# A two-layer decoder on one core: constants queued behind a norm, unread products at the start, and another split of the last stage

## The chip, the cores and the metric

The kernel runs on one core of a Trainium2 chip. The metric is the time of one execution on the device in microseconds (us), lower is better. TensorE is called PE here, VectorE DVE, ScalarE ACT, GpSimd POOL and SyncE SP, as in the profile. PEld is PE's weight load, and a q after a name (SPq) is the queue on which that engine issues transfers.

## The reference

Eight sequences of 128 tokens, 256 wide, pass through two decoder layers. Each layer has self-attention, cross-attention with a context, and a feed-forward, each followed by a residual and a norm without weights. Layer 0's feed-forward has 4-bit weights with low-rank additions; layer 1's is a mixture of 64 experts, of which each token takes the best 8.

```
x = _layernorm(x + _L0_attn_ref(x, Wq, Wk, Wv, Wo))          # 16 heads of 16, causal
x = _layernorm(x + _L0_xattn_ref(x, ctx, ...))
x = _layernorm(x + _L0_ffn_ref(x, ...))                      # 256 -> 1024 -> 256
x = _layernorm(x + _L1_attn_ref(x, w_qkv, w_o))              # 16 heads of 128
x = _layernorm(x + _L1_xattn_ref(x, ctx, ctx))               # 8 heads
x = _layernorm(x + _L1_ffn_ref(x, gate_w, w13, w2))          # 64 experts, the best 8 per token

_layernorm(x) = (x - mean(x)) / sqrt(var(x) + 1e-5)

_L1_ffn_ref(x):
    combine = weights of the 8 best experts of each token, from softmax(x @ gate_w.T)
    out = sum over experts e of combine[:, e] * (silu(x @ w13_e[:128].T) * (x @ w13_e[128:].T)) @ w2_e.T
```

## The kernel before, in words

All arithmetic of the products is in float32, which PE does in two passes; the profile shows each product as two records. The stages follow one another in the order of the reference, and within a stage a planner orders the instructions of DVE, ACT and POOL by priorities and estimated times of its own, while PE's order is mostly written out by hand. Every engine works through its own queue in order. An instruction that waits holds up all that stand behind it on its engine.

**Start.** SP issues the loads of weights and inputs, `wq` and `xT` first (`load`, L118). PE's first work is `project` (L286), which makes queries, keys and values of the first four sequences (tiles `l_p`) from `xT` and `wq`, `wkk`, `wv`. Then a pipeline of scores, softmax, transposes and weighing runs over sequences and head groups (L383). The softmax (L206) takes maxima on DVE (`nm_l`), exponentials on ACT (`l_e`), and scales on DVE (L220). The feed-forward's weights are made beside it: `dequantise` (L231) loads codes (`q_up`) and scales (`sc_up`), and a DVE step at L241 multiplies them to `w_up`.

**Feed-forward of layer 0.** `down` (L418) ends each sequence with a norm. `layernorm` (L173) takes statistics on DVE (`st`, `mv`), the root on POOL in two steps (`rsqrt_eps`, L167: an addition at L170 and a power at L171, tile `rs`), and the last step on DVE (L181). It returns the root's instruction; for the norms before the feed-forward these are kept in `roots`. `transposed` (L184) then turns the normed tiles on PE (`pt_l1a`) for layer 1, whose attention projects each head's q, k and v (L691).

After the feed-forward the program text names constants for routing and for layer 1's cross-attention, all made on POOL: `before`, `iota`, `starts`, `numbers`, `turns`, `rows_16`, `blks_16`, `seen`, and the two halves of `keys` (L602 to L640). In the text they stand behind the last norm. In POOL's queue the planner mixes them with it.

**Expert loop.** Tokens are sorted by expert, 104 visits of 128 columns each multiply with one expert's weights (L1093, L1110), and results go by indirect transfers to `pair_rows` in memory. In between, DVE makes `cw`, the eight weights of each token (`weight`, L1021), and `spread` (L1036) lays the first `ON_PE` = 6 of them on diagonals (`diag`).

**Tail.** After the loop, eight transfers of 1 MB on SP's queue bring back one sequence each as `z`, tokens by 8 results of 256. For each sequence, PE sums the first six results with the diagonals (`moe_sum`, L1176), DVE adds the last two to the residual (L1180) and then PE's sum to it (`moe_r`, L1182). `layernorm` makes `y`, and ACT's queue carries it out (L1185). `r` and `y` take turns in two buffers each of the pool `wk`.

Of the kernel before, what the change touches and what calls it, by code (L numbers as in the profile page):

```python
# [9 lines left out]
F32 = mybir.dt.float32  # L10
# [3 lines left out]
AF = mybir.ActivationFunctionType  # L14
ALU = mybir.AluOpType
AX = mybir.AxisListType

P = 128
B = 8
S = 128  # L20
D = 256
# [12 lines left out]
TOP = 8  # L34
NG = B * S * TOP // P
# [4 lines left out]
MIDDLE = (P - 1) / 2  # L40
# [19 lines left out]
def decoder_kernel(ctx: ExitStack, tc: tile.TileContext, i, out):  # L60
    nc = tc.nc
# [5 lines left out]
    wk = ctx.enter_context(tc.tile_pool(name="work", bufs=2))  # L67
    sm = ctx.enter_context(tc.tile_pool(name="small", bufs=4))
# [22 lines left out]
    def ps_o(name):  # L91
        return ps_of["o"].tile([P, 512], F32, tag="o", name=name)
# [74 lines left out]
    def rsqrt_eps(dst, var):  # L167

        n = dst.shape[1]
        nc.gpsimd.tensor_scalar(dst, var, EPS, None, ALU.add)  # L170
        return nc.gpsimd.tensor_tensor(dst, dst, minus_half[: dst.shape[0], :n], ALU.pow)  # L171

    def layernorm(dst, r, name):  # L173

        st = sm.tile([P, 6], F32, tag="ln_st", name=f"st_{name}")
        nc.vector.bn_stats(st, r)  # L176
        mv = sm.tile([P, 2], F32, tag="ln_mv", name=f"mv_{name}")
        nc.vector.bn_aggr(mv, st)  # L178
        rs = sm.tile([P, 1], F32, tag="ln_rs", name=f"rs_{name}")
        root = rsqrt_eps(rs, mv[:, 1:2])  # L180
        nc.vector.tensor_scalar(dst, r, mv[:, 0:1], rs, ALU.subtract, ALU.mult)  # L181
        return root.ins
# [23 lines left out]
    def softmax(e, s, name):  # L206
# [12 lines left out]
        for a in range(n):  # L219
            nc.vector.tensor_scalar(e[:, a, :], e[:, a, :], inv[:, a : a + 1], None, ALU.mult)  # L220

    w_up = fp.tile([P, 2, FF], F32, name="w_up")
# [50 lines left out]
    with l0, tc.tile_pool(name="l0a", bufs=2) as ap:  # L275
# [102 lines left out]
                project(1, 2 * b + jj)  # L378

        with tc.manual_schedule(engines={nc.tensor.engine}):  # L380
            for part in range(8):
                project(0, part)
            run_pipelined(  # L383
                [(b, jj) for b in range(B) for jj in range(2)], [scores, ahead, turn, weigh, add]
            )
# [8 lines left out]
    roots = []  # L394
# [23 lines left out]
    def down(b):  # L418
        h, bb = b // 4, b % 4
        xb = wk.tile([P, D], F32, tag="xb", name=f"xb_{b}")  # L420

        with tc.issue_after(roots[B - 1]):
            nc.gpsimd.tensor_tensor(xb, x2[b // 2][:, b % 2, :], b_down, ALU.add)
        ps = ps_o(f"down_{b}")
        for f in range(NF):
            nc.tensor.matmul(
                ps[:, :D], hT[h][:, f, bb * S : (bb + 1) * S], w_dn[:, f, :],
                start=(f == 0), stop=(f == NF - 1),
            )
        r = wk.tile([P, D], F32, tag="r", name=f"ff_r_{b}")  # L430
        nc.vector.tensor_tensor(r, ps[:, :D], xb, ALU.add)
        layernorm(x3[b // 2][:, b % 2, :], r, f"l0f_{b}")


    with tc.tile_pool(name="l0x", bufs=2) as ap, tc.manual_schedule(engines={nc.tensor.engine}):
# [149 lines left out]
    with tc.manual_schedule(engines={nc.tensor.engine}):  # L585
# [14 lines left out]
    rp = ctx.enter_context(tc.tile_pool(name="route", bufs=1))  # L600

    before = rp.tile([P, P], F32, name="before")  # L602
    nc.gpsimd.memset(before, 1.0)
    nc.gpsimd.affine_select(
        before, before, pattern=[[1, P]], compare_op=ALU.is_gt, fill=0.0, base=0, channel_multiplier=-1
    )
    iota = rp.tile([P, P], F32, name="iota")
    nc.gpsimd.iota(iota, pattern=[[1, P]], base=0, channel_multiplier=0, allow_small_or_imprecise_dtypes=True)
    starts = rp.tile([P, P], F32, name="starts")
    nc.gpsimd.iota(starts, pattern=[[P, P]], base=0, channel_multiplier=0, allow_small_or_imprecise_dtypes=True)  # L610

    numbers = rp.tile([P, B], F32, name="numbers")
    nc.gpsimd.iota(
        numbers, pattern=[[S, B]], base=0, channel_multiplier=1, allow_small_or_imprecise_dtypes=True
    )
    nc.gpsimd.tensor_scalar(numbers, numbers, 1.0 / (B * S), 1.0, ALU.mult, ALU.add)
    turns = rp.tile([P, TOP], F32, name="turns")
    nc.gpsimd.iota(turns, pattern=[[1, TOP]], base=0, channel_multiplier=0, allow_small_or_imprecise_dtypes=True)
    rows_16 = rp.tile([P, P, TOP], F16, name="rows_16")
    nc.gpsimd.iota(rows_16, pattern=[[1, P], [0, TOP]], base=0, channel_multiplier=0, allow_small_or_imprecise_dtypes=True)  # L620
    nc.gpsimd.tensor_scalar(rows_16, rows_16, -MIDDLE, None, ALU.add)
    blks_16 = rp.tile([P, NG, TOP], F16, name="blks_16")
    nc.gpsimd.iota(blks_16, pattern=[[1, NG], [0, TOP]], base=0, channel_multiplier=0, allow_small_or_imprecise_dtypes=True)
    comb = rp.tile([P, B, NE], F32, name="combine")
    seen = rp.tile([P, B, NE], F32, name="seen")
    nc.gpsimd.memset(seen[:, 0, :], 0.0)


    slot1 = rp.tile([P, B, NE], F32, name="slot1")


    keys_pool = ExitStack()
    kpool = keys_pool.enter_context(tc.tile_pool(name="l1k", bufs=1))
    keys = kpool.tile([P, B, 2, D], F32, name="keys")
    kept = []
    one_at = ident.rearrange("p (j two r) -> p two r j", two=2, r=16)
    for par in range(2):
        m = cp.tile([P, 1], F32, name=f"one_row_{par}")
        nc.vector.reduce_sum(m, one_at[:, 1 - par, 0, :], axis=AX.X)
        nc.gpsimd.tensor_scalar(keys[:, :, par, :], cx, quarter[par], m, ALU.mult, ALU.add)  # L640
        t = cp.tile([P, 1], F32, name=f"kept_{par}")
        nc.vector.tensor_tensor(t, m, rows_of[par], ALU.add)
        kept.append(t)


    x4 = new_stream("x4")
# [19 lines left out]
        layernorm(x4[b // 2][:, b % 2, :], r, f"l1a_{b}")  # L666

    def weigh(st, h, n):

        if n == L1_HEADS - 1:  # L670
            add_heads(4 * h, 0, n)
        ps = ps_o(f"l1_c_{h}_{n}")
        nc.tensor.matmul(ps, ones, st["p"].rearrange("p b k -> p (b k)"), start=True, stop=True)  # L673
        nc.vector.tensor_tensor(st["v"], ps, st["v"], ALU.mult)  # L674
        scaled[h, n] = st["v"]
        if n == L1_HEADS - 1:
            add_heads(4 * h, n, n + 1)
            if h == 0:
                for b in range(1, 4):
                    add_heads(b, 0, L1_HEADS)  # L680
# [349 lines left out]
        nc.vector.reduce_sum(cw[:, b, :], eq, axis=AX.X)  # L1030


    ON_PE = 6
    diag = dgp.tile([P, B, ON_PE, P], F32, name="diag")

    def spread(b):  # L1036
# [130 lines left out]
    zs = []  # L1167
    for b in range(B):
        z = tp.tile([P, TOP, D], F32, tag="z", name=f"z_{b}")
        nc.sync.dma_start(out=z, in_=zv[b])  # L1170
        zs.append(z)
    for b in range(B):
        z = zs[b]
        ps = ps_mm(f"moe_sum_{b}")[:, :D]
        for k in range(ON_PE):
            nc.tensor.matmul(ps, diag[:, b, k, :], z[:, k, :], start=(k == 0), stop=(k == ON_PE - 1))  # L1176

        acc = x5[b // 2][:, b % 2, :]
        for k in range(ON_PE, TOP):
            nc.vector.scalar_tensor_tensor(acc, z[:, k, :], cw[:, b, k : k + 1], acc, ALU.mult, ALU.add)  # L1180
        r = wk.tile([P, D], F32, tag="r", name=f"moe_r_{b}")
        nc.vector.tensor_tensor(r, ps, acc, ALU.add)  # L1182
        y = wk.tile([P, D], F32, tag="y", name=f"y_{b}")
        layernorm(y, r, f"l1f_{b}")
        nc.scalar.dma_start(out=out[b], in_=y)  # L1185


# [60 lines left out]
```

## Time and profile before

Three runs took 901.76, 903.53 and 905.52 us; the median is 903.53.

| | before |
|---|---|
| profiled execution, its own time | 903.73 us |
| its span | 901.9 us |
| PE busy | 820.6 us (91%) |
| DVE busy | 465.0 us (52%) |
| ACT busy | 287.8 us (32%) |
| POOL busy | 228.1 us (25%) |
| mean granted PE clock | 0.95 |
| bytes moved by transfers | 87.63 MB |

The span runs from the first instruction to the last, and the execution's own time has 1.8 us around it. Busy times are sums over stages with different limits, so the timeline of a stage tells more than the shares. A row of a timeline gives the start, the length, the engine, the line, the operation with its output and inputs, how many instructions it stands for, and in brackets how long the engine was idle before it and what ended that.

### The profile page before, as it was taken

To read this page: it belongs to the slowest core of one execution; us is meant where nothing else is said; L and a number is where in the kernel's file an instruction comes from. 1 tells how busy PE (TensorE), PEld (TensorE's weight loads), DVE (VectorE), ACT (ScalarE), POOL (GpSimd) and SP (SyncE) were. 2 spreads that over 40 slices of the span, in tenths; PEclk is the share of its full clock that TensorE was granted. 3 is DMA by queue.
4 is the path that set the end of the run, shared out by engine and by line. 5 is a ranking of instruction groups with operands and counts; after the bars stand their busy time and mean duration, and the time that the engine had idled before them with its cause. 6 is when DMAs were issued, how large, how long until landed. Compare 5 with 4: busy or idle time off the path is not lost. (4 is left out here: it accounts for less than half of the span.)

```text
span 901.9 us, 14220 instructions
## 1 busy us (share of the span) xinstructions
PE 820.6 (91%) x4560; PEld 545.3 (60%) x4560; DVE 465.0 (52%) x1304; ACT 287.8 (32%) x988; POOL 228.1 (25%) x311
## 2 busy tenths in 40 slices
PE   7998998999799999999999999997588888999845
PEld 3555454377455556855556755544488877888844
DVE  2999766431244443244444367665796333433325
ACT  2667353211233332033432033332232322333300
POOL 0010301231500000100005122201566655555522
PEclk9999978799899999999999999998599999999969
DMA  7500030080000000000001000000578888989573
GB/s 224 177 1 1 1 94 0 1 280 0 0 1 0 1 1 1 0 1 0 1 0 47 1 1 13 13 13 13 188 213 286 292 275 240 296 291 295 177 290 157
DMA packets 39105, 87.63 MB, mean 97 GB/s; under 512 B 6128, under 2 KB 15696, under 8 KB 38000
## 3 DMA queue, kind: packets, MB, share of 16 engines
q1 hardware_dynamic: 31728, 68.80, 23.7%
q0 software_dynamic: 6144, 16.79, 5.5%
q10 hardware_dynamic: 1152, 1.05, 0.3%
q8 instruction: 41, 0.67, 0.3%
q14 instruction: 40, 0.33, 0.1%
HBM read 76.13 MB, written 10.49 MB: 96 GB/s over the span
## 5 line engine op out<-in xcount | busy, mean ns | idle before, releaser
L213 ACT ACTIVATE l_e<-l_s,nm_l 128x128 f32<-128x128 f32 x256 | 90.4, 369 | 88.1 <-DVE nm_l L210 87.8
L1093 PE MATMUL moe_gu_few<-cols,w_few 128*128 (+1 forms) x832 | 114.1, 280 | 3.2 <-issue 0.9
L1093 PEld LDWEIGHTS moe_gu_few<-cols,w_few 128*128 128x128 f32 x832 | 102.1, 193 | 10.8 <-issue 9.6
L1123 POOL DMA_INDIRECT pair_rows<-moe_os_few,pairs x64 | 63.2, 988 | 54.2 <-DVE moe_os_few L1122 41.6
L1047 POOL DMA_INDIRECT xg_few<-x_rows,tok_i x60 | 62.3, 1038 | 31.0 <-PE moe_gu_few L1093 11.9
L1110 PE MATMUL moe_o_few<-moe_h_few,w_few 128*128 128x128 f32 x416 | 63.5, 275 | 0.0
L691 PE MATMUL l_k<-xT_l1a,w_qkv 128*128 128x512 f32 x128 | 61.9, 607 | 0.0
L691 PE MATMUL l_v<-xT_l1a,w_qkv 128*128 128x512 f32 x128 | 60.3, 593 | 0.0
L691 PE MATMUL l_q<-xT_l1a,w_qkv 128*128 128x512 f32 x128 | 60.2, 593 | 0.0
L1113 ACT COPY cols<-moe_o_few 128x256 f32 (+1 forms) x104 | 38.9, 374 | 61.4 <-PE moe_oT_few L1120 26.9
L794 ACT ACTIVATE y_e<-y_sT 128x512 f32<-128x512 f32 x64 | 33.0, 603 | 78.9 <-PE y_sT L787 46.3
L674 DVE TENSOR_TENSOR l_vs<-l_c,l_vs 128x512 f32<-128x512 f32 x32 | 22.1, 692 | 68.7 <-PE l_c L673 68.7
L658 PE MATMUL l_y<-w_o,l_vs 128*128 128x256 f32 x256 | 56.9, 381 | 0.0
L220 DVE TENSOR_SCALAR l_e<-l_e,inv_l 128x128 f32<-128x128 f32 x256 | 55.9, 283 | 1.4
L1110 PEld LDWEIGHTS moe_o_few<-moe_h_few,w_few 128*128 128x128 f32 x416 | 54.7, 192 | 0.0
L658 PEld LDWEIGHTS l_y<-w_o,l_vs 128*128 128x128 f32 x256 | 48.2, 190 | 9.8 <-issue 2.8
L1101 ACT ACTIVATE moe_s_few<-moe_gu_few 128x128 f32<-128x128 f32 x104 | 29.1, 280 | 76.5 <-PE moe_gu_few L1093 45.4
L213 ACT ACTIVATION_READ_ACCUMULATOR l_e<-l_s,nm_l 128x1 f32 x256 | 53.0, 207 | 0.0
L1103 DVE TENSOR_TENSOR moe_h_few<-moe_gu_few,moe_s_few 128x128 f32<-128x128 f32 x104 | 29.8, 287 | 39.9 <-ACT moe_s_few L1101 28.4
L1072 DVE COPY cols<-moe_xT_few 128x256 f32<-128x256 f32 x64 | 26.6, 419 | 45.5 <-PE moe_o_few L1110 19.8
L210 DVE TENSOR_REDUCE nm_l<-l_s 128x4 f32<-128x512 f32 x64 | 43.2, 685 | 10.1 <-PE l_s L706 8.2
L699 ACT COPY l_vs<-l_v 128x512 f32<-128x512 f32 x32 | 18.8, 586 | 80.3 <-PE l_v L691 80.3
(264 smaller groups left out, 1381.0 us busy)
## 6 DMA issues: line engine op xcount, KB each, us to landing
w_few<-in_experts SPq DMA_DIRECT2D x104, 384.0 KB
z<-pair_rows SPq DMA_DIRECT2D x8, 1024.0 KB
w_qkv<-in_w_qkv SPq DMA_DIRECT2D x8, 768.0 KB
w_o<-in_w_o SPq DMA_DIRECT2D x1, 2048.0 KB
xT<-in_xT SPq DMA_DIRECT2D x2, 512.0 KB
x<-in_x SPq DMA_DIRECT2D x4, 256.0 KB
cx<-in_ctx SPq DMA_DIRECT2D x1, 1024.0 KB
q_up<-in_up_qT SPq DMA_DIRECT2D x4, 256.0 KB
```

Of the source, the lines that this page charges most:

```text
L210: nc.vector.tensor_reduce(nm, s, AX.X, ALU.max, negate=True)
L213: nc.scalar.activation(e[:, a, :], s[:, a, :], AF.Exp, bias=nm[:, a : a + 1], scale=1.0, accum_out=sums[:, a : a + 1],)
L220: nc.vector.tensor_scalar(e[:, a, :], e[:, a, :], inv[:, a : a + 1], None, ALU.mult)
L658: nc.tensor.matmul(py[:, :D], scaled[b // 4, m][:, b % 4 * S : (b % 4 + 1) * S], w_o[:, m, :], start=(m == 0), stop=(m == L1_HEADS - 1),)
L691: nc.tensor.matmul(ps, w_qkv[:, k, c, n, :], xT[h][:, k, :], start=(k == 0), stop=(k == 1))
L794: nc.scalar.activation(e, tiles[j], AF.Exp)
L1047: nc.gpsimd.indirect_dma_start(out=x, out_offset=None, in_=xd, in_offset=bass.IndirectOffsetOnAxis(ap=tok_i[:, g : g + 1], axis=0), bounds ...
L1093: mm = nc.tensor.matmul(ps[:, a, :], ws[v][:, at : at + P], cols[:, k, bass.ds(o + P, P)], start=(k == 0), stop=(k == 1),)
L1103: nc.vector.tensor_tensor(hid, ps[:, 1, :], s, ALU.mult)
L1110: nc.tensor.matmul(ps[:, c, :], ws[v][:, at : at + P], hs[v], start=True, stop=True)
L1113: cp = nc.scalar.copy(cols[:, :, bass.ds(o, P)], ps)
L1123: inst = nc.gpsimd.indirect_dma_start(out=zd, out_offset=bass.IndirectOffsetOnAxis(ap=pairs[:, g : g + 1], axis=0), in_=o, in_offset=None, ...
```

## The change

It has five parts.

- The constants on POOL move into a function, `make_constants`. It is called in layer 1's attention, before the second head's weighing, and `tc.issue_after(roots[-1])` lets none of its instructions stand ahead of the last root on POOL's queue. `roots` now holds the feed-forward's roots too.
- `keep_busy` multiplies two constants ten times into a PSUM tile that nobody reads, ahead of the first `project`.
- `ON_PE` becomes 5: PE sums five of the eight results, DVE three.
- The first sequence's `z` comes in two transfers, results 0 to 4 and results 5 to 7.
- The last norm is written out: statistics on DVE and the root on POOL as before, then a third POOL step (`shift` = −mean × root), and the final step on ACT, `y = r × root + shift`. `r` and `y` have four buffers each, in the tail's pool.

```diff
+    def keep_busy(tile, n):
+        for _ in range(n):
+            nc.tensor.matmul(tile[:, :P], ident, ones, start=True, stop=True)
...
         with tc.manual_schedule(engines={nc.tensor.engine}):
+            keep_busy(ps_o("wait_x"), 10)
             for part in range(8):
                 project(0, part)
...
-        layernorm(x3[b // 2][:, b % 2, :], r, f"l0f_{b}")
+        roots.append(layernorm(x3[b // 2][:, b % 2, :], r, f"l0f_{b}"))
...
-    nc.gpsimd.memset(before, 1.0)
...
-        nc.gpsimd.tensor_scalar(keys[:, :, par, :], cx, quarter[par], m, ALU.mult, ALU.add)
+        one_row.append(m)
...
+    def make_constants():
+        nc.gpsimd.memset(before, 1.0)
...
+        nc.gpsimd.iota(rows_16, pattern=[[1, P], [0, TOP]], base=0, channel_multiplier=0, allow_small_or_imprecise_dtypes=True)
+        nc.gpsimd.tensor_scalar(rows_16, rows_16, -MIDDLE, None, ALU.add)
...
+        for par in range(2):
+            nc.gpsimd.tensor_scalar(keys[:, :, par, :], cx, quarter[par], one_row[par], ALU.mult, ALU.add)
...
     def weigh(st, h, n):
+        if (h, n) == (0, 1):
+            with tc.issue_after(roots[-1]):
+                make_constants()
...
-    ON_PE = 6
+    ON_PE = 5
...
-        nc.sync.dma_start(out=z, in_=zv[b])
+        for at in (slice(0, ON_PE), slice(ON_PE, TOP)) if b == 0 else (slice(0, TOP),):
+            nc.sync.dma_start(out=z[:, at], in_=zv[b, :, at])
...
-        r = wk.tile([P, D], F32, tag="r", name=f"moe_r_{b}")
+        r = tp.tile([P, D], F32, tag="r", bufs=4, name=f"moe_r_{b}")
         nc.vector.tensor_tensor(r, ps, acc, ALU.add)
-        y = wk.tile([P, D], F32, tag="y", name=f"y_{b}")
-        layernorm(y, r, f"l1f_{b}")
+        st = sm.tile([P, 6], F32, tag="ln_st", name=f"st_l1f_{b}")
+        nc.vector.bn_stats(st, r)
+        mv = sm.tile([P, 2], F32, tag="ln_mv", name=f"mv_l1f_{b}")
+        nc.vector.bn_aggr(mv, st)
+        rs = sm.tile([P, 1], F32, tag="ln_rs", name=f"rs_l1f_{b}")
+        rsqrt_eps(rs, mv[:, 1:2])
+        shift = sm.tile([P, 1], F32, tag="ln_shift", name=f"shift_l1f_{b}")
+        nc.gpsimd.tensor_scalar(shift, mv[:, 0:1], rs, -1.0, ALU.mult, ALU.mult)
+        y = tp.tile([P, D], F32, tag="y", bufs=4, name=f"y_{b}")
+        nc.scalar.activation(y, r, AF.Identity, bias=shift, scale=rs)
         nc.scalar.dma_start(out=out[b], in_=y)
```

## The prediction

> **What bounds the kernel now.** I read the page's slices first: TensorE (PE) is busy 91% of the span, so a gain has to come from stretches where PE waits or runs slowly. There are three of them where the change acts: the start, the end of layer 0's feed-forward (near 230 us), and the tail (after 862 us). I read the timeline in each.
>
> Feed-forward's end, timeline of 226 to 236 us (start, length, engine, line, operation, in brackets the idle time before it and what ended it; the l_k and l_v rows from the view of PE alone):
>
> ```profile
> 227.30 0.18 DVE L178 BATCH_NORM_AGGREGATE mv_l0f<-st_l0f 128x2 f32<-128x6 f32 x1
> 227.59 1.88 PE L691 MATMUL l_q<-xT_l1a,w_qkv 128*128 128x512 f32 x4
> 228.98 1.02 POOL L623 IOTA blks<- 128x512 f16 x1
> 230.09 0.22 POOL L170 TENSOR_SCALAR rs_l0f<-mv_l0f 128x1 f32<-128x1 f32 x1
> 230.38 2.80 POOL L621 TENSOR_SCALAR rows<-rows 128x1024 f16<-128x1024 f16 x1
> 233.15 0.57 POOL L171 TENSOR_TENSOR rs_l0f<-rs_l0f,minus_half 128x1 f32<-128x1 f32 x1
> 233.75 0.45 DVE L181 TENSOR_SCALAR x<-ff_r,mv_l0f,rs_l0f 128x256 f32<-128x256 f32 x1 [5.31 <-POOL rs_l0f L171]
> 234.26 0.90 PE L194 MATMUL pt_l1a<-ident,x 128*128 128x128 f32 x3 [4.79 <-DVE x L181]
> 234.95 3.62 PE L691 MATMUL l_k<-xT_l1a,w_qkv 128*128 128x512 f32 x4
> 238.37 2.02 PE L691 MATMUL l_v<-xT_l1a,w_qkv 128*128 128x512 f32 x4
> ```
>
> The reader is to see that the last norm's statistics are ready at 227.48, while its two POOL steps stand among the constants and end at 233.72. PE waits 4.79 us for them and comes back slow: four l_k products take 3.62 us, where the four of l_q, of the same shape, took 1.88 (granted clock 0.50 in the stretches from 232 to 238, 1.00 before).
>
> Start, timeline of 0 to 32 us:
>
> ```profile
> 5.91 5.67 PE L300 MATMUL l_p<-xT,wq 128*128 128x512 f32 x8 [5.91 <-DMA xT<-in_xT]
> 9.46 0.34 PEld L300 LDWEIGHTS l_p<-xT,wq 128*128 128x128 f32 x1 [0.52 <-issue]
> 10.13 0.19 PEld L300 LDWEIGHTS l_p<-xT,wq 128*128 128x128 f32 x1 [0.33 <-issue]
> 20.69 1.11 SPq L237 DMA_DIRECT2D sc_up<-in_up_scT x2
> 22.47 0.87 DVE L220 TENSOR_SCALAR l_e<-l_e,inv_l 128x128 f32<-128x128 f32 x4
> ```
>
> PE starts when xT lands at 5.91 and is slow until about 10.0 (weight loads fall from 0.34 to 0.19 us and their spacing from 0.85 to 0.43; the clock column reads 1.00 already from 5 to 10, so here I go by these durations, which are those of the stretch at 0.50). The last two rows matter for the DVE's new order below.
>
> Tail, timeline of 860 to 902 us, then the stretches of 2 us (the busy time of PE, PEld, DVE, ACT, POOL; clock; DMA share; GB/s):
>
> ```profile
> 868.70 23.33 PE L1176 MATMUL moe_sum<-z,diag 128*128 128x256 f32 x96 [10.44 <-DMA z<-pair_rows]
> 884.14 0.41 DVE L181 TENSOR_SCALAR y<-moe_r,mv_l1f,rs_l1f 128x256 f32<-128x256 f32 x1 [2.40 <-DMA out<-y]
> 893.10 0.41 DVE L181 TENSOR_SCALAR y<-moe_r,mv_l1f,rs_l1f 128x256 f32<-128x256 f32 x1 [0.98 <-POOL rs_l1f L171]
> 896.04 0.41 DVE L181 TENSOR_SCALAR y<-moe_r,mv_l1f,rs_l1f 128x256 f32<-128x256 f32 x1 [0.99 <-POOL rs_l1f L171]
> 898.45 0.41 DVE L181 TENSOR_SCALAR y<-moe_r,mv_l1f,rs_l1f 128x256 f32<-128x256 f32 x1 [0.98 <-POOL rs_l1f L171]
> ...
> 884.00:886.00 2.00, 2.00 (x11) 1.77 (x10) 1.86 (x5) 0.00 (x0) 0.00 (x0) 1.00 0.97 399
> 886.00:888.00 2.00, 2.00 (x11) 1.74 (x11) 0.98 (x5) 0.00 (x0) 0.78 (x2) 1.00 0.16 53
> ```
>
> The last z has landed at about 886.2 and PE ends at 892.03, but DVE ends at 898.86. DVE sets the end, one sequence each 2.95 us, with 1.0 us in each spent waiting for POOL's root.
>
> **The change part by part.**
>
> *Constants behind the last norm.* The changed program's POOL order has both steps of rs_l0f for the last sequence ahead of all constants; nothing else there moves, and the order of PE, DVE and ACT near 230 us stays. The new times: statistics at 227.48, POOL's first step 0.30 (start to start, as for earlier sequences), root 0.57, so about 228.45. DVE's copy of xT_l1a ends at 228.44, so x runs from 228.5 to 228.9. PE's l_q products last until about 229.3, so the three transposes follow with no gap and l_k comes at full speed. By spacing of full-speed products (0.43 us each, four per projection, so 1.7): transposes to 229.7, l_k to 231.4, where l_v starts. Before it started at 238.37: 7.0 us. This is 4.8 of wait and some 2.1 of slow clock. From 242 to 380 PE is busy without a gap (40.0 of 40 us in each stretch), so the saving is carried on. What is queued behind: some 15 us of constants now end near 244 on POOL, whose next other work in the trace is at 360; their readers come after 380. Both ends: 4.8 (the clock falls anyway) and 7.2. I take 7.0.
>
> A rule that speaks against this: the Trainium skill, "GPSIMD Engine Reference", section "1. Specifications", has POOL and VectorE share SBUF interfaces, with contention for some DVE instructions. The two keys steps (4.2 us each) ran beside an almost idle DVE; now they lie beside the first softmaxes (l_e at 0.28 us an instruction, 0.2 spacing). No row of this trace shows the two together. By the rows alone the cost is 0. By the rule, if those DVE instructions took twice their time, DVE's 8.0 busy us of 18 (242 to 260) would become 16 at most, still under PE's 18; a late first l_e might cost PE 1 to 2 us. I take 0 and keep 2 for the range.
>
> *Unread products.* Ten 128x128 products are 20 records on PE. They need `ones`, done at 1.89, so they start at 1.95. A 512-column record took 0.85 us slow, so 128 columns take about 0.21, and 20 take 4.3: to 6.25, or 0.35 us after xT lands. The row for full speed is the start itself: 4.1 us after PE's first product (5.91 to 10.0); after the gap at 234.26 it was again 4.1. From 1.95 that gives 6.05, so the real products run at full speed from 6.25. Before, the 4.1 us did the work of 2.05 us; so PE is at the same product 2.05 − 0.35 = 1.7 us earlier. Against it stands the rule of the Trainium skill, "TensorE: Matmul & The Clock Gate", "What's actually happening": the activity window of 3413 ns is free-running. By it full speed could come after one to two windows, at 5.4 to 8.8, and the gain would be between 1.7 and about 0.4 us. The lower end is −0.35 (no effect on the clock). wk and wv are no obstacle: SP's lane waits put their landings near 8.4 and 9.1, and PE now needs them at 9.7 and 13.1.
>
> What is late next: the scheduler now puts DVE's first w_up step (L241, before at 30.52) directly behind the first l_e group. It waits for sc_up, issued at 20.69 to 21.80; the trace shows no landing, and I estimate 23.0 to 24.3 from bytes moved (524 KB for q_up and sc_up, some 0.45 MB moved from 20 to 23 us beside other loads). DVE would be there at 23.3 − 1.7 = 21.6, and everything queued behind it (the next inv_l, maxima and l_e, and ACT and PE after those) waits about 2 us. Part is paid back, as w_up's 0.6 us no longer falls into the saturated stretch after 30 us (DVE busy 9.8 of 10). I count 1.0 us for this part, from −0.4 to 1.7.
>
> *The tail.* ON_PE 6 to 5 makes PE's 12 records per sequence 10: at 0.213 us (half of 0.43), 2.56 becomes 2.13. That is under the landing interval of z: 871.18 (DVE's second wait) to 886.2 is six tiles, 2.5 us each. DVE gains one accumulation per sequence (0.46, start to start), loses L181 (0.33) and its wait for the root (1.0). In the changed order a sequence is STT 0.39, aggregate 0.15, two dependent STT 0.92, add 0.45, statistics 0.33: 2.24 us, also under 2.5. So the tail follows the transfers. The last z: 886.2, plus 0.4 because one or two more 128 KB outputs travel among the z tiles at 420 GB/s: 886.6. Then PE 2.13 and 0.1 to hand over; add 0.45, statistics 0.46, aggregate 0.27; POOL 0.30, root 0.60, and the new shift 0.30 (nearest row L170; at most the root's 0.57); ACT 0.40 (nearest row: copies of 128x256 at 0.37; at most 0.6, the 128x512 row). Sum 5.0: y at 891.6. Before, 898.86, so 7.3 us. The end stays 3.04 us behind the last y in both.
>
> Four buffers for r and y remove the 2.40 us wait on out<-y; the first output took 7.6 us to land, and the fifth y now comes 9 or so after its issue, so it hardly waits. Splitting the first z brings PE's start forward by about 1 us, which only helps it to catch up with the landings after its slow start: worth 0. One diag product less per sequence (0.28 us) in the expert loop lies beside DVE's idle half: 0. I take 7.0 for the tail, from 3.5 (DVE's interval stays near 3 us for some sequences, or outputs slow z) to 8.
>
> **Sum.** 7.0 + 1.0 + 7.0 = 15.0. The profiled execution's own time is 903.73 (span 901.9 and 1.8 around it), 0.2 above the median of 903.53: 888.7, or 888.5 against the median.
>
> **Rivals.**
> - *The start is hidden* (the products do not do what they are for): DVE waits for sc_up, or the clock rises late. 889.5 to 890. For it: the in-order wait above.
> - *The tail gets a new bound.* If DVE or the transfers of outputs hold the tail at 2.8 to 3 us per sequence, it gains 3.5: 892. For it: 2.24 against 2.5 is a small margin, and out<-y took 7.6 us beside z. Against it: DVE's remaining work is measured.
> - *Contention of the late constants* in layer 1's first heads: 2 us, 890.5.
> - *Slower: the expert loop.* The scheduler regroups DVE's diag and eq steps between the hid products for the 104 visits. If hid came later by t in each, the loop would grow by 104t: it eats the gain at 0.14 us and is slower by over 0.5% from 0.19 us (19.5 us), giving 908 and above. Against it: DVE has eight steps fewer, is busy 8 of 20 us in most stretches there, and PE waited for DVE less than 7 us in the whole loop.
>
> **How the numbers follow.** All three parts as summed: 0.62, at 886 to 891. Start hidden: 0.15. Tail bound anew: 0.11. Contention: 0.04. Several of these at once with a smaller loss in the loop, 899 to 908: 0.04. Expert loop beyond that: 0.04. The range takes in the start's and tail's ends and the runs' spread of about 2 us each way: 884.5 to 894.5. A measurement can tell about 0.5% (4.5 us) from no change: faster than 899.0 has 0.92, within 0.5% 0.04, slower 0.04.
>
> **What would show it.** Right: PE's gap before pt_l1a is gone and l_k takes 1.88; the first l_p weight loads are 0.19; in the tail PE waits for z in each sequence and ACT's y follows the last landing by 5 us. Wrong: DVE's first w_up row with an idle time over 2 us (start), DVE's tail rows still 2.9 us apart, l_e rows above 0.4 us beside keys, or PE waits on moe_h in the expert loop.

## The result, and the profile after

The changed kernel takes 899.58 us (median of 7 runs, 897.77 to 901.11), the kernel before 904.92 on the same chip (7 runs, 901.76 to 905.82). The ratio is 0.9951, with a 95% interval of 0.9932 to 0.9970. A second measurement on another chip gave 895.23 against 901.70, ratio 0.9925 (0.9895 to 0.9955). It is faster, but by 5.3 and 6.5 us in the medians instead of the 15 forecast; 888.5 and the whole range up to 894.5 were missed.

The profiled execution took 901.11 us, the slowest of the seven. Its span is 899.4 us, 2.5 below that of before. I followed the distance between the two traces from mark to mark:

| mark | before, us | after, us | after minus before |
|---|---|---|---|
| first scores `l_s` | 18.83 | 17.60 | −1.2 |
| layer 1's first `l_q` | 227.59 | 231.6 | +4.0 |
| layer 1's first `l_c` | 246.3 | 244.0 | −2.3 |
| last `y_sT` of layer 1's cross-attention | 615.2 | 615.8 | +0.6 |
| last scatter of the expert loop | 860.1 | 859.7 | −0.4 |
| end of the span | 901.9 | 899.4 | −2.5 |

So the start, counted at −1.0, cost 4.0. The constants brought 6.3. Some 2.9 of that was lost again in cross-attention, where nothing was changed. The tail, counted at −7.0, brought 2.1 from the last scatter on, and 2.7 from the first z issue on (38.1 to 35.4 us).

**Feed-forward's end**, timeline of 210 to 250 us, the rows that answer to those of before:

```profile
231.87 0.56 POOL L171 TENSOR_TENSOR rs_l0f<-rs_l0f,minus_half 128x1 f32<-128x1 f32 x1
232.46 0.47 DVE L181 TENSOR_SCALAR x<-ff_r,mv_l0f,rs_l0f 128x256 f32<-128x256 f32 x1
233.31 0.49 PE L194 MATMUL pt_l1a<-ident,x 128*128 128x128 f32 x3
233.63 1.88 PE L708 MATMUL l_k<-xT_l1a,w_qkv 128*128 128x512 f32 x4
...
239.55 4.12 POOL L655 TENSOR_SCALAR keys<-cx,quarter,one_row 128x2048 f32<-128x2048 f32 x2
240.64 3.30 DVE L220 TENSOR_SCALAR l_e<-l_e,inv_l 128x128 f32<-128x128 f32 x4
243.99 1.13 PE L690 MATMUL l_c<-l_e,ones 128*128 128x512 f32 x2 [0.72 <-DVE l_e L220]
```

The root is no longer among the constants, the transposes have no wait, and four `l_k` products take 1.88 us instead of 3.62. This is the step as predicted. The last three rows are its price: beside the two `keys` steps four `l_e` instructions take 3.30 us instead of 0.88, and PE waits 0.72 us. Two of the four are long, 1.03 and 1.92 us; they end at 241.67 and 243.76, 0.1 us after a `keys` step each (241.59 and 243.67).

**Start**, timeline of 0 to 40 us (the last two PE rows from the view of PE alone):

```profile
1.95 4.64 PE L225 MATMUL wait_x<-ones,ident 128*128 128x128 f32 x20 [1.95 <-POOL ones L100]
6.53 3.83 PE L305 MATMUL l_p<-xT,wq 128*128 128x512 f32 x8
...
21.24 0.88 DVE L220 TENSOR_SCALAR l_e<-l_e,inv_l 128x128 f32<-128x128 f32 x4
...
25.77 0.69 DVE L246 SCALAR_TENSOR_TENSOR w_up<-q_up,sc_up 128x512 f32<-128x512 int32 x1 [3.65 <-DMA sc_up<-in_up_scT]
...
27.37 1.12 PE L344 MATMUL l_eT<-ident,l_e 128*128 128x128 f32 x4 [4.30 <-DVE l_e L220]
28.28 3.11 PE L305 MATMUL l_p<-xT,wq 128*128 128x512 f32 x4
```

The unread products do their work: eight real ones take 3.83 us instead of 5.67. But DVE reaches `w_up` at 22.1, waits 3.65 us for `sc_up`, and the second `l_e` group stands behind it. PE stops for 4.30 us and comes back slow: four `l_p` products take 3.11 us, where four of the same shape had taken 1.98 just before.

**Tail**, PE's rows and the last rows of DVE and ACT from the timelines of 860 to 900 us, then stretches of 2 us with the columns of the prediction:

```profile
868.26 13.89 PE L1195 MATMUL moe_sum<-z,diag 128*128 128x256 f32 x50 [11.37 <-DMA z<-pair_rows]
882.47 2.40 PE L1195 MATMUL moe_sum<-z,diag 128*128 128x256 f32 x10 [0.33 <-DMA z<-pair_rows]
886.78 6.24 PE L1195 MATMUL moe_sum<-z,diag 128*128 128x256 f32 x20 [1.91 <-DMA z<-pair_rows]
890.79 0.42 DVE L1201 TENSOR_TENSOR moe_r<-moe_sum,x 128x256 f32<-128x256 f32 x1 [2.60 <-PE moe_sum L1195]
895.83 0.60 ACT L1211 ACTIVATE y<-moe_r,shift_l1f,rs_l1f 128x256 f32<-128x256 f32 x1 [1.30 <-POOL shift_l1f L1209]
...
866.00:868.00 2.00, 0.00 (x0) 0.00 (x0) 0.00 (x0) 0.00 (x0) 0.00 (x0) 0.50 0.95 339
868.00:870.00 2.00, 1.74 (x4) 1.50 (x5) 0.13 (x1) 0.00 (x0) 0.00 (x0) 0.50 0.96 367
886.00:888.00 2.00, 1.22 (x5) 1.08 (x6) 1.51 (x5) 0.60 (x1) 0.51 (x2) 0.87 0.84 313
888.00:890.00 2.00, 2.00 (x6) 1.61 (x5) 0.19 (x1) 0.60 (x1) 0.88 (x2) 0.50 0.06 22
```

Before, the first z was issued at 863.78, here at 864.03. The stretch of before that answers to the first one:

```profile
866.00:868.00 2.00, 0.00 (x0) 0.00 (x0) 0.00 (x0) 0.00 (x0) 0.00 (x0) 0.50 1.00 418
```

So the transfers stood at 418 GB/s from 866 on, and at 53 after 886. Now they start at 339 and 367, and still move 313 after 886. The seventh sequence's `z` comes late, PE waits 1.91 us for it, the clock falls to 0.50, and the last 20 records take 6.24 us.

**Cross-attention**, stretches of 2 us. First the kernel before, in which the same products run about 2 us later, then the changed one:

```profile
562.00:564.00 2.00, 1.16 (x6) 0.69 (x5) 1.75 (x9) 1.84 (x7) 0.00 (x0) 1.00 0.00 0
564.00:566.00 2.00, 2.00 (x11) 1.00 (x8) 1.92 (x4) 0.81 (x2) 0.93 (x1) 1.00 0.04 8
566.00:568.00 2.00, 2.00 (x38) 1.00 (x36) 0.76 (x2) 0.00 (x0) 0.00 (x0) 1.00 0.00 0
```

```profile
562.00:564.00 2.00, 2.00 (x8) 1.05 (x7) 2.00 (x4) 0.64 (x2) 0.76 (x1) 0.80 0.00 0
564.00:566.00 2.00, 2.00 (x19) 0.98 (x21) 0.68 (x2) 0.00 (x0) 0.00 (x0) 0.50 0.00 0
566.00:568.00 2.00, 2.00 (x32) 1.12 (x28) 0.51 (x1) 0.00 (x0) 0.00 (x0) 0.84 0.00 0
```

In both traces PE waits 0.84 us for ACT's `r_e` just before this. In the kernel before the clock stays at 1.00, in the changed one it falls for 3.4 us. Summed over such stretches from the first of cross-attention to the last, PE stood 3.4 us at half clock before and 10.2 after. That is 3.4 us of time, about what the table shows lost there. Nothing shows it to be a cost of the change: in the twenty profiles of this study this time at half clock runs from 0 to 13.7 us, and it is 10.2 or 13.7 in seventeen of them, only_start and only_tail below included. So the profile of before was a lucky one here.

A number for this is used below: the time lost to the half clock in an execution, its span times one minus its mean granted clock. It is an upper figure, since half clock costs nothing while PE waits: of the 30.7 us at half clock after 624 us, in both traces, PE was busy for 17.5 to 17.7. In the second measurement the changed kernel's eleven runs lie between 887.29 and 899.40 us, and their time lost to half clock between 41.6 and 53.0. Without it their standard deviation is 2.0 us, with it 3.4.

### The profile page after: what moved, and what is told of

Read it like the earlier page. It is cut to its first block, busy times and chain, and to the rows that moved or that the text cites. A ratio compares the mean times of both kernels' runs of the same rounds, so it can differ in the third digit from the quotient of the medians.

```text
span 899.4 us, 14258 instructions
## 1 busy us (share of the span) xinstructions
PE 823.2 (92%) x4564; PEld 550.0 (61%) x4564; DVE 467.5 (52%) x1296; ACT 293.2 (33%) x996; POOL 232.6 (26%) x319
## 5 line engine op out<-in xcount | busy, mean ns | idle before, releaser
L708 PE MATMUL l_k<-xT_l1a,w_qkv 128*128 128x512 f32 x128 | 60.1, 592 | 0.0
L220 DVE TENSOR_SCALAR l_e<-l_e,inv_l 128x128 f32<-128x128 f32 x256 | 58.3, 292 | 1.4
L691 DVE TENSOR_TENSOR l_vs<-l_c,l_vs 128x512 f32<-128x512 f32 x32 | 22.1, 692 | 67.4 <-PE l_c L690 67.4
L716 ACT COPY l_vs<-l_v 128x512 f32<-128x512 f32 x32 | 18.8, 586 | 78.3 <-PE l_v L708 78.3
```

What stands on the lines that cost most here:

```text
L708: nc.tensor.matmul(ps, w_qkv[:, k, c, n, :], xT[h][:, k, :], start=(k == 0), stop=(k == 1))
```

## Experiments

Times of different chips are not compared with each other, only ratios to the kernel before on the same chip. Marks within a trace are.

### The parts one at a time

Three kernels are the kernel before with one part of the change each: the ten unread products, the constants held back, or the tail (`ON_PE` = 5, the first z in two transfers, the last norm written out, four buffers). The fourth is the changed kernel without the unread products:

```diff
-            keep_busy(ps_o("wait_x"), 10)
```

> The ten unread products alone, everything else as before. Theory 1 (the products shift DVE's order, and its first w_up step then waits for sc_up in front of the softmax): 3 to 5.5 us slower than before, with an idle time of 3 us or more before the first w_up row on DVE, a PE gap of about 4 us near 23 us, and the first project rows at full speed. Rival A (the wait seen after the change was one execution's late transfer and the order does not matter): 1 to 2 us faster than before. Rival B (the faster start is paid back by the softmax and nothing reaches the end): within 1 us of before.

> The constants behind the last norm alone. Theory 1: PE's wait before the last transposes and its slow spell after it go (7.0 us), and about 1 us comes back because the softmax's first l_e group stands behind keys on the shared port: 5.5 to 6.5 us faster at the first l_c product, and the same at the end within 3 us either way for clock dips in the cross-attention. Rival (the late constants cost more than the wait they replace): less than 3 us faster.

> The tail alone: five results on PE, first z in two transfers, the last step on ACT, four buffers. Theory 1 (DVE no longer sets the end, the last two z tiles do, which land close together and late and let PE's clock fall): 1.5 to 4 us faster than before, with PE waiting for z ahead of the last two sequences and their 20 records taking 5 us or more instead of 4.3. Rival (the landings are 2.5 us apart and the changed execution's were an exception): 6 to 8 us faster.

> The change without the ten unread products. Theory 1: the start is as before (DVE's order too), so 4 to 6 us faster than the change and 8 to 11 us faster than before: about 894 to 896. Rival A: 1 to 2 us slower than the change, about 901. Rival C (most of the missing gain was lost in the cross-attention and the loop, not at the start): within 1.5 us of the change.

| kernel | us (runs) | ratio to before (878.42 us, 33 runs), 95% | seen in the trace |
|---|---|---|---|
| only_start | 881.48 (22) | 1.0035 (1.0018 to 1.0051) | layer 1's first `l_q` at 227.7, in the others 223.6 to 223.8 |
| only_consts | 873.92 (12) | 0.9950 (0.9932 to 0.9968) | first `l_c` at 236.2; 243.1 in only_tail |
| only_tail | 871.23 (6) | 0.9911 (0.9889 to 0.9933) | 32.4 us from the first z issue to the end; 39.0 in only_start, 39.3 in only_consts |
| no_start | 865.62 (5) | 0.9850 (0.9830 to 0.9871) | tail 32.4 us |

The unread products alone make the kernel slower: 3.1 us by the medians, 4.0 up to the first `l_q` by the traces, as in the changed kernel. DVE's order is the changed one there too, and `w_up` stands at 26.15 after a wait of 3.17 us for `sc_up`. The constants move `l_c` by 6.8 us. The time gained 4.5, so part was lost further on; as in the changed kernel the half clock is what varies there, but I did not follow it mark by mark. The tail is worth 6.6 to 6.9 us on this chip by the traces (7.2 by the medians, the rival's size in only_tail), where it was 2.7 in the changed kernel's first profile. no_start gains 12.8 us, more than the 8 to 11 of its theory 1, and about what constants and tail gain one at a time (4.5 and 7.2). PE's rows of no_start's tail, beside the one row of the old tail in only_start:

```profile
835.02 16.34 PE L1194 MATMUL moe_sum<-z,diag 128*128 128x256 f32 x60 [10.15 <-DMA z<-pair_rows]
851.75 2.40 PE L1194 MATMUL moe_sum<-z,diag 128*128 128x256 f32 x10 [0.39 <-DMA z<-pair_rows]
854.55 2.40 PE L1194 MATMUL moe_sum<-z,diag 128*128 128x256 f32 x10 [0.40 <-DVE x L1198]
```

```profile
849.14 23.69 PE L1182 MATMUL moe_sum<-z,diag 128*128 128x256 f32 x96 [11.89 <-DMA z<-pair_rows]
```

No wait is over 0.40 us and no group of ten takes more than 2.40. The late z is missing.

### Undoing the two losses, and the split of the first z

All of these hold the whole change. start_held keeps DVE's order at the start as it was:

```diff
-        nc.vector.tensor_reduce(nm, s, AX.X, ALU.max, negate=True)
+        maxima_of[name] = nc.vector.tensor_reduce(nm, s, AX.X, ALU.max, negate=True).ins
...
-        nc.vector.scalar_tensor_tensor(w, q, -7.5, sc, ALU.add, ALU.mult)
+        with tc.issue_after(maxima_of["l0_1_1"]):
+            nc.vector.scalar_tensor_tensor(w, q, -7.5, sc, ALU.add, ALU.mult)
```

held_keys8 is start_held with `keys` in short steps, held_one_z is start_held with the first z whole:

```diff
-            nc.gpsimd.tensor_scalar(keys[:, :, par, :], cx, quarter[par], one_row[par], ALU.mult, ALU.add)
+            for b in range(B):
+                nc.gpsimd.tensor_scalar(keys[:, b, par, :], cx[:, b, :], quarter[par], one_row[par], ALU.mult, ALU.add)
```

```diff
-        for at in (slice(0, ON_PE), slice(ON_PE, TOP)) if b == 0 else (slice(0, TOP),):
-            nc.sync.dma_start(out=z[:, at], in_=zv[b, :, at])
+        nc.sync.dma_start(out=z, in_=zv[b])
```

> The changed kernel itself, beside new variants. Theory T1 (the first unread products cost 4 us through VectorE's order, constants give 7 less about 1 of contention, and the tail gives 7.5 unless the last z tiles land late): the ratio to the kernel before is 0.989 where the tail's last z tiles land as evenly as in no_start (PE waits of 0.4 us for them), 0.994 where they do not (PE waits of 1.9 us). Theory T2 (the unread products at the start, or anything else of the whole change that the single parts lack, spoil the tail): 0.994 here too, with a tail of 39.7 us from the last scatter to the end, whatever the start.

> The whole change, with VectorE's first w_up step held behind the maxima of the second head group of layer 0, so that VectorE's order at the start is that of the kernel before. Theory S1 (the wait for sc_up in VectorE's new order is what turned the gain of the unread products into a loss): the 4.0 us lost up to 230 us become a gain of 1 to 1.7 us, so 5 to 6 us below after_again, and 1 to 1.5 us below the whole change without the unread products (ratio about 0.983). Theory S2 (the loss has another cause, such as PE's clock after its early start, or the softmax chain that is late whatever the order): within 2 us of after_again.

> As start_held, and each of the two keys steps of GpSimd, 128x2048, split into eight of 128x256. Theory K1 (a VectorE step from SBUF to SBUF stands still until the running GpSimd step ends, so short ones let it through): the first l_e group takes about 0.9 to 1.5 us instead of 3.30, PE no longer waits before l_c, 0.7 to 1 us below start_held. Theory K2 (the port is lost to VectorE while GpSimd has anything of this kind to do, however short): l_e still takes over 3 us, no gain, and GpSimd's fixed cost makes the keys longer.

> As start_held, but the first z tile in one transfer, as before the change. By the prediction the split is worth nothing at the end (it only brings PE's first products forward): within 0.5 us of start_held. Theory Z1 (the split costs a place in the transfers' order or a queue's slot, so the last tiles land late): 0.5 to 1.5 us below start_held. Theory Z2 (the early start of PE is what lets it keep up): 0.5 to 1 us above.

| kernel | us (runs) | ratio to before (901.70 us, 14 runs), 95% | median lost to half clock, us | the rest, us |
|---|---|---|---|---|
| before | 901.70 (14) | | 47.2 | 854.1 |
| after_again | 895.23 (11) | 0.9925 (0.9895 to 0.9955) | 47.4 | 847.8 |
| start_held | 890.60 (4) | 0.9871 (0.9816 to 0.9927) | 45.3 | 845.1 |
| held_keys8 | 883.76 (4) | 0.9836 (0.9772 to 0.9899) | 41.5 | 844.1 |
| held_one_z | 887.22 (4) | 0.9867 (0.9807 to 0.9927) | 42.9 | 844.7 |

(Both last columns are medians over the runs, so they add up only roughly.)

after_again stands between its two theories (0.989 and 0.994) and does not tell them apart. start_held is 4.6 us below the changed kernel, close to the 5 to 6 of theory S1; S2's 2 us are too few. Timeline of its start:

```profile
22.52 1.48 PE L347 MATMUL l_eT<-ident,l_e 128*128 128x128 f32 x8
...
23.84 1.89 PE L308 MATMUL l_p<-xT,wq 128*128 128x512 f32 x4
...
29.39 0.68 DVE L249 SCALAR_TENSOR_TENSOR w_up<-q_up,sc_up 128x512 f32<-128x512 int32 x1
```

`w_up` runs at 29.39 with no wait, PE has no gap before `l_eT`, and `l_p` comes at full speed. The order was the loss. The other profiles agree, though the ranges overlap: the first `l_q` of layer 1 stands at 227.3 to 232.6 us with the unread products and the changed order (six profiles, mean 229.8), at 223.7 to 228.5 without the products (seven, 225.0), and at 220.7 to 226.7 with the products and the old order (seven, 222.7).

held_keys8, timeline of 225 to 245 us:

```profile
229.34 8.81 POOL L659 TENSOR_SCALAR keys<-cx,quarter,one_row 128x256 f32<-128x256 f32 x16
230.44 1.33 DVE L222 TENSOR_SCALAR l_e<-l_e,inv_l 128x128 f32<-128x128 f32 x4
...
232.91 1.02 PE L694 MATMUL l_c<-l_e,ones 128*128 128x512 f32 x2
```

The sixteen short steps take twice as long on POOL as the two long ones (8.81 against 4.12), but `l_e` passes between them in 1.33 us and PE does not wait. From the first `l_q` to the first `l_c` it is 11.5 us here and 12.4 in start_held: 0.9 us, in the range of K1. The larger step of the medians, 6.8 us, is more than that: the half clock, which comes and goes between runs, fell by 3.8, and the last column falls by 1.0. held_one_z differs from start_held by 0.4 us in the last column, too little to read.

### All three edits, wider operands, and no unread products

all_three is the changed kernel with the three edits. all_three_pad also fills four low-rank operands up to 128 rows:

```diff
-    up_a = load("up_a", [RANK, D], i["up_aT"], pool=fl)
...
+    def load_padded(name, width, src):
+        t = fl.tile([P, width], F32, name=name)
+        nc.gpsimd.memset(t, 0.0)
+        nc.sync.dma_start(out=t[:RANK], in_=src)
+        return t
+    up_a = load_padded("up_a", D, i["up_aT"])
...
```

> The whole change with three edits: VectorE's first w_up step held as in start_held, the keys steps split as in held_keys8, the first z in one transfer as in held_one_z. If the three act at different places and add up (start, 230 us, tail), 13 to 16 us below the kernel before, ratio 0.983 to 0.986 with TensorE's clock as it falls on average (44 to 47 us of the span lost to half clock), and 0.5 to 1.5 us below held_keys8. Rival: one z transfer brings PE's start in the tail later and gives nothing: same as held_keys8.

> As all_three, but the four low-rank operands of layer 0's feed-forward weights (up_a, up_b, dn_a, dn_b) stand in tiles of 128 rows filled up with zeros, so the 24 products ab_up and ab_dn use 128 rows of the array instead of 16; the results are the same and each product streams as many columns as before. Between 104 and 127 us TensorE was busy without a gap in the kernel before and its clock yet fell to 0.5 for 4 to 20 us. Theory R (the clock follows the share of the array in use, so products of 16 rows count as idle): half-clock time from 100 to 180 us falls from 20 to 34 us to under 10, and the time by 4 to 8 us. Theory W (only waits of TensorE let the clock fall): no difference to all_three beyond 1 us, the half-clock time from 100 to 180 stays at 20 to 34 us.

> The change without the unread products, beside the two above on one chip. Theory S1 (with VectorE's order kept, the unread products gain 1 to 1.7 us at the start): all_three is 2 to 3.5 us below this one, of which 1 to 1.7 come before the first w_up step's place (30 us), the rest from the keys and the tail. Theory S0 (the unread products are worth nothing, since PE waits for loads and VectorE soon after): the two are at the same time up to 220 us once the half-clock time is taken off.

| kernel | us (runs) | ratio to before (900.25 us, 9 runs), 95% | lost to half clock, us: median (range) |
|---|---|---|---|
| no_start_again | 889.07 (5) | 0.9888 (0.9850 to 0.9926) | 43.5 (38.1 to 46.4) |
| all_three | 883.98 (5) | 0.9828 (0.9801 to 0.9854) | 38.8 (35.2 to 44.2) |
| all_three_pad | 881.84 (5) | 0.9790 (0.9753 to 0.9828) | 33.6 (31.5 to 38.0) |

all_three gains 16.3 us by the medians, the size that was forecast for the change. Of this, 5.1 us is time lost to half clock (43.9 in the kernel before on this chip, median), which varies from run to run; the rest fell by 9.6 (854.8 to 845.2). It is 5.1 us below no_start_again, more than S1's 2 to 3.5, but 4.7 of that is half clock too. Its profile and no_start_again's have the same time at half clock up to 220 us, 20.5 us, and its first `l_q` stands at 221.2 against 223.8: 2.7 us for the unread products once DVE keeps its order. Another pair does not show it: at 23.9 us of half clock held_keys8_again, run later, has 224.2, and no_start and only_tail have 223.7. The means above differ by 2.3 us, and by about 1.5 with half of the time at half clock taken off. So the products gain something, of S1's size (1 to 1.7) or a little more.

all_three_pad had a question of its own. From 116 to 124 us the kernel before keeps PE busy without a gap, and the clock is still at half (stretches of 4 us, and a PE row of that time):

```profile
116.00:120.00 4.00, 4.00 (x9) 2.74 (x10) 2.42 (x4) 1.02 (x4) 0.00 (x0) 0.50 0.67 180
120.00:124.00 4.00, 4.00 (x13) 2.52 (x12) 3.33 (x10) 2.09 (x6) 0.00 (x0) 0.50 0.52 147
...
119.46 2.07 PE L244 MATMUL ab_dn<-dn_b,dn_a 16*128 16x256 f32 x4
```

With 128 rows instead of 16, PE stood 17.1 us at half clock from 100 to 180 us, against 20.5 in all_three; from 100 to 120 it was 0 against 4.2. Theory R expected under 10, theory W 20 to 34. Over the runs the time lost falls by 5 us, but the rest rises by 3 (848.1 against 845.2), and the total by 2.1 only. Neither theory is settled by this.

### Is the late z chance, the whole change, or the split?

Four known kernels ran once more, one run each, then three with the first z whole (the diff of held_one_z, made on the changed kernel and on no_start):

> A third look at the changed kernel, for its tail. Chance (the late landing is a matter of the execution): from the first z issue to the end 32.3 to 35.4 us, without the wait of 1.9 us in about half of such looks. Tied (something in the whole change makes it): 34 to 35.4 us with the wait of 1.9 us again.

> A second look at start_held. Chance: transfers begin at the rate of the other kernels (330 to 360 GB/s in the second stretch of 2 us after the first z issue, not 252), and 32.3 to 35 us from the first issue to the end. Tied: 252 GB/s and 35 us again.

> A second look at held_keys8, whose tail has the same instructions as the changed kernel's. Chance: 32.3 to 35.4 us. Tied: 32.4 us again, since this kernel did not show the late landing.

> A second look at the tail alone. Chance: 32.3 to 35.4 us from the first z issue to the end. Tied to the unread products or to the constants: 32.3 us again.

> The changed kernel, with the first z in one transfer as before the change. Split at fault: 32 to 33 us from the first z issue to the end, transfers over 400 GB/s from the second stretch of 2 us on, and about 2 us below the changed kernel. Chance whatever the split: 34 to 35.5 us in about half of such looks.

> The same again: with the split at fault 32 to 33 us in every look; by chance alone 34 to 35.5 us in about half of them.

> The change without the unread products and with the first z in one transfer: with the split at fault 32 to 33 us from the first z issue to the end; by chance alone 34 to 35.5 us in about half of such looks.

The first four took 894.97, 892.34, 893.28 and 896.25 us beside 903.86 of the kernel before, the last three 870.53, 870.56 and 868.14 beside 877.13. Single times say little here, and the changed kernel did not run beside the last three; the tails are read from the traces. Time from the first z issue to the end, in every profile of this study:

| tail | profiles | us |
|---|---|---|
| old | before, only_start, only_consts | 38.1, 39.0, 39.3 |
| new, first z in two transfers | only_tail, no_start, held_keys8, no_start_again, start_held_again | 32.4, 32.4, 32.4, 32.5, 32.6 |
| the same, late | after_again, start_held, only_tail_again, held_keys8_again, after, after_third | 34.1, 35.0, 35.0, 35.1, 35.4, 35.5 |
| new, first z in one transfer | all_three_pad, after_one_z, no_start_one_z, all_three, after_one_z_again, held_one_z | 32.0, 32.3, 32.4, 32.7, 33.0, 33.1 |

held_keys8 and only_tail, good at first, were late in their second profile, and start_held the other way round. So the late landing is not tied to the whole change. All six late profiles have the split. If the six had fallen blindly among the seventeen, all would lie among the eleven split ones in 1 of 27 cases (462 of 12376 ways). Three of the whole ones, and two good split ones, come from chips with a faster expert loop, where no profile was late. Without those it is 84 of 924 ways, 1 of 11. That the split brings the late landings is therefore favoured by the counts, not shown.

What the split does to the transfers is in every trace. The second and third stretch of 2 us after the first z issue (846.3 and 857.7), first of all_three, then of after_third:

```profile
848.30:850.30 2.00, 0.00 (x0) 0.00 (x0) 0.00 (x0) 0.00 (x0) 0.00 (x0) 0.50 1.00 422
850.30:852.30 2.00, 1.13 (x3) 0.98 (x4) 0.74 (x2) 0.00 (x0) 0.00 (x0) 0.50 1.02 430
```

```profile
859.70:861.70 2.00, 0.00 (x0) 0.00 (x0) 0.00 (x0) 0.00 (x0) 0.00 (x0) 0.50 0.98 261
861.70:863.70 2.00, 1.73 (x4) 1.49 (x5) 0.00 (x0) 0.00 (x0) 0.00 (x0) 0.50 0.90 233
```

From 2 to 4 us after the first issue the six whole profiles move 406 to 434 GB/s, the eleven split ones 261 to 350. The first part does come earlier: PE starts 4.2 to 4.4 us after the issue in ten of the eleven, not 4.9 to 5.0. But DVE, which needs the second part, starts its first accumulation at 5.5 to 5.8, later than with the whole z (5.2 to 5.4). In three of the late profiles it starts at 8.2 to 8.5; in the other three a z near the end is late. The slow first microseconds alone do not decide it: the five split profiles that were not late move 325 to 350 GB/s there, and these other three 340 to 343.

## Why the prediction was wrong, point by point

Two steps failed: the unread products, where DVE's wait for `sc_up` and the clock that PE lost by it turned −1.0 into +4.0, and the tail, where −7.0 became −2.7 because DVE's interval was mis-sized and a late z, 2.9 us, was not counted.

**Where the bound lies.** Right: the three places were the ones where the change acts, and each part did what the diff says.

**Constants, −7.0.** Right in size: −6.3 in the changed kernel up to the first `l_c`, −6.8 on its own. The contention beside it was priced at 0, with 2 kept as a rival of 0.04; it came. The Trainium skill, "GPSIMD Engine Reference", section "1. Specifications", has POOL and VectorE share interfaces to SBUF, the on-chip memory, with contention for some VectorE instructions. The trace agrees, and more strictly than the doubling that I worked out: two of DVE's four short instructions did not take twice their time, they stood until POOL's long one ended (3.30 us for 0.88 in all). It cost PE 0.72 us here, and splitting `keys` gave 0.9 back. (The prediction's 4.2 us for each `keys` step is the two together, 2.16 and 2.04.)

**Unread products, −1.0 with a range to +0.4.** This step failed, by 5.0 us. Three terms of it:
- That PE would be at full speed when xT is there was nearly right: the spacing of products is 0.65 us at 6.53 and 0.43 from 7.18 on, so full speed came at about 7.0 by estimate (a slow product took 0.85), not 6.05, and within the 5.4 to 8.8 of the estimate from the window. Eight products took 3.83 us, and the first scores stand at 16.8 to 18.5 us in every profile with the unread products, mean 17.6, against 18.8 to 20.1, mean 19.7, without. This is the 1.7 counted, or a little more.
- The wait for `sc_up` was seen, but its landing was put at 23.0 to 24.3; DVE's `w_up` started at 25.77 (25.6 to 27.0 in the other profiles with this order). The wait was 3.65 us, not about 2.
- PE was to wait about 2 us behind it. It waited 4.30 us, and what was left out is that it lost its full clock: 3.4 to 10.2 us at half speed between 20 and 40 us in every profile with this order, none without. That is 1.7 to 5.1 us of time. The prediction used the clock's slow return at 0 and at 234 us, and did not ask for it a third time where it made PE wait anew.

The sum had a gap of its own: 1.7 earlier, about 2 of wait and at most 0.6 paid back make 0.3, and not the 1.0 that was taken. The rival "start hidden" named the wait but stopped at a gain of 0. Its own number for a loss, −0.4 in the range, was far too small.

**The tail, −7.0.** The mechanism was right, and some sizes were off. DVE's interval is 2.42 to 2.45 us in the steady stretch of fourteen of the seventeen new tails (up to 2.8 in the other three), not 2.24. One sequence of after_one_z, timeline of DVE:

```profile
852.76 0.42 DVE L1199 TENSOR_TENSOR moe_r<-moe_sum,x 128x256 f32<-128x256 f32 x1
853.22 0.43 DVE L1201 BATCH_NORM_STATS2 st_l1f<-moe_r 128x6 f32<-128x256 f32 x1
853.57 0.47 DVE L1197 SCALAR_TENSOR_TENSOR x<-z,pair_weight,x 128x256 f32<-128x256 f32 x1
853.95 0.17 DVE L1203 BATCH_NORM_AGGREGATE mv_l1f<-st_l1f 128x2 f32<-128x6 f32 x1
854.07 1.01 DVE L1197 SCALAR_TENSOR_TENSOR x<-z,pair_weight,x 128x256 f32<-128x256 f32 x2
855.21 0.42 DVE L1199 TENSOR_TENSOR moe_r<-moe_sum,x 128x256 f32<-128x256 f32 x1
```

The last two accumulations and the start of the next sum are 1.14 us apart (854.07 to 855.21), not 0.92; the other starts are as counted. So DVE sets the pace wherever z comes on time. PE's ten records need 2.40 from the first start to the last end, not 2.13. In no_start the last `moe_r` starts 26.3 us after the first issue, where some 25 was forecast. The chain behind it is longer too: 3.2 us from there to the end of `y`, not 2.8, of which 0.2 is ACT's `y` (0.60 us, not 0.40). The end stays 3.0 us behind the last `y`, as counted. So y ends at 29.5 and the span at 32.4, where 27.8 and 30.9 were forecast. This is a gain of 5.7 on the trace of before, and 6.5 to 6.9 on the other old tails. On top came the late landings, 1.7 to 3.1 us in six profiles (2.9 in the changed kernel's first), all three of the changed kernel among them. They go with the split of the first z, which the prediction costed at nothing because PE would only start sooner; that the split makes them is not shown. It did not ask what two smaller transfers do to the queue.

**The rivals.** Contention and a new bound in the tail both came, small. The expert loop, the case on the slower side, did not: first to last `moe_gu` takes 201.6 us before and 199.7 after. That the clock would fall in places the change does not touch was no rival at all.

**The sum.** Up to the first `l_c`, start and constants made −2.3 where −8.0 was summed. The tail adds −2.7 from the first issue on. Against the profile of before, cross-attention's half clock took 2.9 back. Over the runs, the time lost to half clock is the same before and after (47.2 and 47.4), although 2.1 of the constants' 7.0 was half clock to be saved.

## What to carry to other kernels

Filling an idle engine before its inputs arrive pays only if no in-order queue behind it now has an instruction ahead of its transfer; one pinned step was worth 4.6 us here. If work that is moved off a critical wait holds up short instructions of the engine that now runs beside it, as `keys` did with `l_e`, cutting it into short steps can help, at a price on its own engine. Before a transfer that bounds a stage is split for a head start, look at the rate of the first microseconds.

## What the runs showed of the hardware

- PE's clock also falls where PE hardly waits. The half-clock time in one place comes in steps: 3.4, 6.8 or 10.2 us between 20 and 40 us, or 3.4 and 6.8 in cross-attention. In all twenty traces every stretch at half clock, but for the one that the end of the span cuts, is a whole number of such steps long, from 3.4 to 34.1 us. The Trainium skill, "TensorE: Matmul & The Clock Gate", section "What's actually happening", has a free-running window of 3413 ns and a fall after about one idle window. The step agrees with the window. The fall does not need an idle one: a wait of 0.84 us is followed by half clock in one trace and not in another, and from 116 to 124 us the clock is at half while PE is busy 8.00 of 8 us.
- This sets the spread of the times. In three profiles with the same start (start_held, held_keys8, held_one_z) the first `l_q` stands at 226.7, 221.4 and 220.7 us, with 34.1, 20.5 and 20.5 us at half clock before it. Half of the 13.6 us is 6.8; the difference is 5.3 and 6.1.
- Two of four DVE instructions on `l_e` stood still beside POOL steps of 2.06 us (1.03 and 1.92 us instead of 0.29); between POOL steps of 0.55 us the longest took 0.51.
- ACT's final step of 128x256 with a bias and a scale for each row took 0.60 us in every profile that has it.
